# One scan per pair of channels over all 1024 tokens, and products by C of 8 tokens by 8 pairs

## The chip, the cores and the metric

The kernel runs on one core of one Trainium2 chip. The metric is the device time of one execution in microseconds, the median of several runs. Engines: TensorE (PE) multiplies and loads its weights (PEld), VectorE (DVE), ScalarE (ACT), GpSimd (POOL), and SyncE (SP), whose queue issues all DMAs.

## The reference

Sixteen samples of 256 channels by 1024 tokens go through an attention layer and then a selective state-space layer. The change is inside the recurrence of the second:

```python
def step(h, inp):
    d_t, B_t, C_t, u_t = inp
    dA = jnp.exp(d_t[..., None] * A)
    h = dA * h + (d_t * u_t)[..., None] * B_t[:, None, :]
    y = jnp.einsum('bdn,bn->bd', h, C_t)
    return (h, y)
```

It runs over 1024 tokens for 512 channels with 64 states each. `y` then goes through a gate and an output projection.

## The kernel before

**Work and tiles.** The 128 partitions hold the 64 states of two channels, a pair. A sample's 512 channels are four groups `k` of 128, each of four `q` of 32 channels, each of 16 pairs. Tokens come in two stretches `t` of 512. A unit is two pairs (`i` from 0 to 7, `e` 0 and 1) over one stretch; 8 units are a block, 256 units a sample, 4096 all.

**One unit.** `load` brings `du` (delta times u), broadcast over the states, 6 units ahead, and B, C and the pieces of delta where they are due. `inputs` (L904) multiplies du by B on POOL, 4 ahead. `decay` (L913) spreads delta over the states with one matmul per pair, each into a PSUM bank, and L916 turns it into exponentials on ACT, 2 ahead. `scan` (L926) runs the recurrence on DVE, one instruction per pair, and writes a slot of the state buffer. In the second stretch a scan starts from the last column of the first, which L951 saved.

**One block.** `outputs` multiplies the 16 slots of a full state buffer by C. `cd` holds C, spread by L939 so that a 128x32 weight has 4 tokens by 2 channels in its own eight columns (its other columns are zero) and four such weights add into 32 output rows. Each matmul (L967) takes 4 tokens of 16 slots as 64 moving columns; four groups of rows `g` are filled in turn. The result holds all combinations of tokens, of which the equal ones are wanted: ACT copies it out (L974, `y2`), and `turned` (L955) picks them with matmuls by parts of the identity into the other half of the bank `yb`. ACT copies that (L981, `yo`) and SP stores it.

**Order.** PE, ACT, DVE and POOL run in the order of the program text. The loop over units issues, for unit n: load(n + 6), inputs(n + 4), the scans of n, decay(n + 2), a share of the side work (the next sample's attention and projections, the last sample's gate), one step of each generator in `running`, and, at `i` = 0, a new `outputs` for the block just done, with its first step. Before, a block's products take seven steps: 32 matmuls at `i` = 0, 16 at each of `i` = 1 to 6; at `i` = 7 the last turn and `yo`.

**Buffers.** Two state buffers h0 and h1 take turns from block to block. A buffer is taken anew, as one tile, by the first scan of a block, which so waits for all readers of its former content. `aps` has four PSUM banks for decays.

Of the kernel before, what the change touches and what calls it, by code (L numbers as in the profile page):

```python
# [19 lines left out]
P = 128  # L20
C = 256
KC = C // P
L = 1024
# [10 lines left out]
TB = 512  # L34
NT = L // TB
SLOTS = 16
UNITS = ND * NT * 4 * 8

# [14 lines left out]
def attention_then_scan_kernel(  # L53
# [35 lines left out]
    aps = pool("aps", 4, space=PSUM)  # L89
# [5 lines left out]
    alone = cycle((mm, aps, aps))  # L95
    beside = {"scan": False}

    def psum(name, dims=P):
        src = mm if beside["scan"] else next(alone)
        return src.tile([P, HL], F32, name=name, tag="mm" if src is mm else "a")[:dims]  # L100
# [4 lines left out]
    def psum3(name):  # L105
        src = next(three) if beside["scan"] else next(alone)
        return src.tile([P, HL], F32, name=name, tag={mm: "mm", accp: "av"}.get(src, "a"))
# [7 lines left out]
    def hs(h):  # L115
        return ts(h, HL)
# [63 lines left out]
    turn = const.tile([P, 4, 2, 16], F32, name="turn")  # L180
    grid = ident.rearrange("p (m e j) -> p e j m", e=4, j=2)
    for e in range(4):
        nc.vector.tensor_copy(turn[:, e], grid[:, e])
# [27 lines left out]
    cd = hst.tile([P, TB // 16, P], F32, name="cd", tag="cd")  # L211
# [376 lines left out]
    def scan_inputs(b):  # L588
# [154 lines left out]
        dus = dram.tile([ND * NT * P, TB], F32, name="dus", tag="dus")  # L743
        dpv = dps.rearrange("(k q e p x) t -> k p e q x t", k=ND, q=4, e=2, p=3)
        duv = dus.rearrange("(k t d) c -> k d t c", k=ND, t=NT)
# [21 lines left out]
        for d in range(ND):  # L767
# [17 lines left out]
            nc.sync.dma_start(duv[d], du.rearrange("d (t c) -> d t c", t=NT))  # L785
# [20 lines left out]
    def gate_and_store(b):  # L806
# [62 lines left out]
        (b, t, k, q, i)  # L869
        for b in range(B) for t in range(NT) for k in range(ND) for q in range(4) for i in range(8)  # L870
# [4 lines left out]
    def load(n):  # L875
        b, t, k, q, i = units[n]
        st = state[b]
        if (k, q, i) == (0, 0, 0):
            bt = blk.tile([P, TB], F32, name="bt", tag="bt")
            ct = blk.tile([P, TB], F32, name="ct", tag="ct")  # L880
            for v, lo in ((bt, 0), (ct, NS)):
                src = st["rows"][lo : lo + NS, ts(t, TB)]
                nc.sync.dma_start(v, src.unsqueeze(1).to_broadcast([NS, 2, TB]))
            blocks[b, t] = {"bt": bt, "ct": ct}
        if i == 0:
            pieces = blk.tile([P, TB], BF16, name="pieces", tag="pieces")
            for e in range(2):
                src = st["dps"][ds(((k * 4 + q) * 2 + e) * 48, 48), ts(t, TB)]
                nc.sync.dma_start(pieces[ds(64 * e, 48)], src)
            blocks[b, t, k, q] = pieces  # L890
        du = dutp.tile([P, 2, TB], F32, name="dub", tag="dub")
        src = st["dus"][ts(k * NT + t, P)].rearrange(
            "(q j i e) c -> q i j (e c)", q=4, j=2, i=8
        )[q, i]
        nc.sync.dma_start(
            du.rearrange("p e c -> p (e c)"),
            src.unsqueeze(0).to_broadcast([NS, 2, 2 * TB]),
        )
        loaded[n] = du

    def inputs(n):
        b, t = units[n][:2]
        v, bt = loaded[n], blocks[b, t]["bt"]
        nc.gpsimd.tensor_tensor(v, v, bt.unsqueeze(1).to_broadcast([P, 2, TB]), ALU.mult)  # L904

    def decay(n):
        b, t, k, q, i = units[n]
        pieces = blocks[b, t, k, q]
        decays[n] = [aps.tile([P, TB], F32, name="a", tag="a") for _ in range(2)]
        for e in (1, 0):  # L910
            a, r = decays[n][e], ds(64 * e, 48)
            w = pick[r, i].rearrange("p n j -> p (n j)")
            nc.tensor.matmul(a, w, pieces[r], start=True, stop=True)  # L913
        for e, a in enumerate(decays[n]):
            at = 64 * k + 16 * q + 2 * i + e
            nc.scalar.activation(a, a, AF.Exp, scale=acol[:, at : at + 1])  # L916

    def scan(n, e):
        b, t, k, q, i = units[n]
        if (i, e) == (0, 0):  # L920
            if (t, k, q) == (0, 0, 0):
                now["last"] = blk.tile([P, DI // 2], F32, name="last", tag="last")
            now["h", q % 2] = hst.tile([P, SLOTS, TB], F32, name=f"h{q % 2}", tag=f"h{q % 2}")
        at = 64 * k + 16 * q + 2 * i + e
        first = now["last"][:, at : at + 1] if t else 0.0
        nc.vector.tensor_tensor_scan(  # L926
            now["h", q % 2][:, 2 * i + e, :], decays[n][e], loaded[n][:, e, :], first,
            ALU.mult, ALU.add,
        )
        if e == 1:  # L930
            del decays[n], loaded[n]
# [3 lines left out]
    def spread_c(b, t, some):  # L935
        ct = blocks[b, t]["ct"].rearrange("p (a c e) -> p a c e", c=4, e=4)
        for c in some:
            for j in range(2):
                nc.scalar.activation(  # L939
                    cd[:, :, 40 * c + j : 40 * c + j + 7 : 2], ct[:, :, c],  # L940
                    AF.Identity, scale=par[:, j : j + 1],
                )
# [4 lines left out]
    def outputs(b, t, k, q):  # L947
        hbuf = now["h", q % 2]
        out4 = yb[:, 256:].rearrange("p (j a m e) -> p a e j m", a=2, j=2, e=4)
        if t == 0:  # L950
            nc.scalar.copy(now["last"][:, ds(64 * k + 16 * q, 16)], hbuf[:, :, TB - 1])  # L951
        def turned(half, y2):
            for e in range(4):
                for s in range(4):
                    nc.tensor.matmul(  # L955
                        out4[32 * s : 32 * s + 16, half, e],
                        y2[:, 64 * s + e : 64 * s + 64 : 4], turn[:, e],
                        start=True, stop=True,
                    )

        y2 = None
        for half in range(2):
            for s in range(4):
                for c in range(4):
                    for g in range(4):
                        at = 128 * s + 64 * half + 16 * g + 4 * c
                        nc.tensor.matmul(  # L967
                            yb[ts(g, 32), ts(s, 64)],
                            cd[:, at // 16, ts(c, 32)], hbuf[:, :, at : at + 4],
                            start=(c == 0), stop=(c == 3),  # L970
                        )
# [3 lines left out]
                if s == 0 and half == 1:  # L975
                    turned(0, y2)
                if (half, s) != (0, 0):
                    yield
        turned(1, y2)
        yo = blk.tile([P, 256], F32, name="yo", tag="yo")  # L980
        nc.scalar.copy(yo, yb[:, 256:])  # L981
        for _ in range(3):
            yield
        to = state[b]["ys"][ds(k * P + 32 * q, 32), ts(t, TB)].rearrange(
            "(j i) (s c) -> s i j c", j=2, s=4
        )
        for s in range(4):
            nc.sync.dma_start(  # L988
                to[s], yo[32 * s : 32 * s + 16].rearrange("p (j c) -> p j c", j=2)
            )  # L990
# [29 lines left out]
    for n, (b, t, k, q, i) in enumerate(units):  # L1020
# [114 lines left out]
```

## Time and profile before

| | us |
|---|---|
| median of 3 runs | 13334.93 (13334.85 to 13353.89) |
| span of the profiled execution | 13355.7 |
| first scan starts, last scan ends | 385, 13308 |
| TensorE clock granted (mean, 1 is full) | 0.790 |
| exponentials L916, busy | 5060.9 |
| products by B on POOL L904, busy | 9690.4 |
| products by C, L967: matmuls, weight loads, busy | 3207.6, 2525.7 |
| copies y2 (L974, 1024) and yo (L981, 512), busy | 385.3, 193.1 |

"Busy" is the time in which at least one instruction of the group ran. A group's line ends with the idle time of its engine just before these instructions, and what ended it. In the slices of the page each digit is a tenth of 40 equal stretches of the span:

```profile
PE   7687878878788787887878878787787877878788
DVE  3899999999999999999999999999999999999998
PEclk8886878878788687887878878797786878879755
```

The 40 slices look alike: after the first sample's preparation the same loop runs to the end.

### The profile page before, as it was taken

The page shows a single profiled execution, that of the slowest core. Times are in us where ns is not written, and L with a number is a line of the kernel's source. Part 1 is how long each engine was busy: PE and PEld are TensorE (multiplying, and loading weights), DVE is VectorE, ACT ScalarE, POOL GpSimd, SP SyncE. Part 2 cuts the span into 40 slices and gives each one's busy share as a digit, 9 for nine tenths or more (in the row PEclk, how much of TensorE's full clock was granted, in tenths as well). Part 3 has the DMA queues.
Part 4 walks back from the last instruction along what each step waited for, and adds up shares of the span by engine and source line. Part 5 has one row for each costly group of instructions (what it writes and reads, how often), then busy time and mean ns, then how long its engine had stood idle before and what let it go on. Part 6 is the DMA issues. An engine that isn't in the chain of part 4 may idle for free. (4 is left out here: it accounts for less than half of the span.)

```text
span 13355.7 us, 429794 instructions
## 1 busy us (share of the span) xinstructions
PE 10665.6 (80%) x186800; PEld 5305.6 (40%) x186800; DVE 12217.1 (91%) x11652; ACT 7891.8 (59%) x13941; POOL 9695.2 (73%) x4105
## 2 busy tenths in 40 slices
PE   7687878878788787887878878787787877878788
PEld 3243343433434334343344433444344343433444
DVE  3899999999999999999999999999999999999998
ACT  3565665656656566565665656566565665656654
POOL 0676777777777777777767767687786877767798
PEclk8886878878788687887878878797786878879755
DMA  1566666675666766666666666666666666676676
GB/s 59 191 212 229 197 210 221 212 236 194 220 219 200 232 200 215 217 205 230 205 216 213 206 225 209 230 210 207 220 215 235 200 208 218 207 233 199 216 253 220
DMA packets 1002092, 2820.53 MB, mean 211 GB/s; under 512 B 176194, under 2 KB 319811, under 8 KB 1000196
## 3 DMA queue, kind: packets, MB, share of 16 engines
q1 hardware_dynamic: 1000196, 2793.03, 62.9%
q8 instruction: 1460, 23.92, 0.7%
q14 instruction: 436, 3.57, 0.1%
HBM read 2513.82 MB, written 261.62 MB: 208 GB/s over the span
## 5 line engine op out<-in xcount | busy, mean ns | idle before, releaser
L904 POOL TENSOR_TENSOR dub<-dub,bt 128x1024 f32<-128x1024 f32 x4096 | 9690.4, 2382 | 3605.4 <-DMA dub<-dus 3139.7
L916 ACT ACTIVATE a<-a,acol 128x512 f32<-128x512 f32 x8192 | 5060.9, 659 | 4086.9 <-PE a L913 4075.1
L926 DVE TENSOR_TENSOR_SCAN h<-a,last,dub 128x512 f32<-128x512 f32 x4096 | 4934.2, 1262 | 180.4 <-POOL dub L904 56.0
L926 DVE TENSOR_TENSOR_SCAN h<-a,dub 128x512 f32<-128x512 f32 x4096 | 4691.0, 1203 | 346.1 <-issue 124.9
L913 PE MATMUL a<-pieces,pick 48*128 48x512 bf16 x8192 | 2941.0, 454 | 2011.5 <-DVE h L926 1929.4
L967 PEld LDWEIGHTS yb<-h,cd 128*32 128x32 f32 x131072 | 2525.7, 131 | 3234.3 <-issue 2194.3
L967 PE MATMUL yb<-h,cd 128*32 128x64 f32 x131072 | 3207.6, 255 | 214.7 <-ACT yo L981 103.1
L913 PEld LDWEIGHTS <-pick 48*128 48x128 bf16 x8192 | 501.6, 95 | 1446.0 <-issue 1166.2
L427 PE MATMUL s_ps<-k,q 32*64 32x512 f32 x4096 | 830.7, 614 | 97.4 <-DVE mx L408 97.4
L955 PEld LDWEIGHTS yb<-turn,y 128*16 128x16 f32 x32768 | 456.1, 121 | 550.1 <-ACT y L974 305.6
L974 ACT COPY y<-yb 128x256 f32<-128x256 f32 x1024 | 385.3, 376 | 474.1 <-PE yb L967 467.7
L955 PE MATMUL yb<-turn,y 128*16 128x32 f32 x32768 | 552.1, 215 | 133.7 <-ACT y L974 133.4
L408 DVE TENSOR_REDUCE mx<-s_ps 128x1 f32<-128x512 f32 x1024 | 644.8, 674 | 9.7 <-PE s_ps L427 9.7
L495 PE MATMUL st_ps<-sp 33*128 33x512 f32 x2048 | 625.6, 650 | 0.1
L483 PE MATMUL av<-pt,vv 128*64 128x512 f32 x2048 | 621.9, 688 | 4.6 <-ACT sums L472 3.3
L503 ACT ACTIVATE pt<-st_ps 128x512 f32<-128x512 f32 x1024 | 557.5, 607 | 57.5 <-PE st_ps L495 56.7
L680 PE MATMUL g_ps<-w,xp 128*128 128x256 f32 x1536 | 517.1, 482 | 0.0
L680 PEld LDWEIGHTS g_ps<-w,xp 128*128 128x128 f32 x1536 | 400.6, 327 | 201.2 <-issue 169.5
L427 PEld LDWEIGHTS s_ps<-k,q 32*64 32x64 f32 x4096 | 193.8, 130 | 708.5 <-DVE mx L408 701.3
L666 DVE SCALAR_TENSOR_TENSOR u<-up,cwh,u 128x1024 f32<-128x1024 f32 x192 | 420.6, 2191 | 24.5 <-ACT u L658 24.2
L852 PE MATMUL m_ps<-w,xs 128*128 128x256 f32 x1024 | 319.0, 461 | 11.9 <-DVE xs L827 11.9
L495 PEld LDWEIGHTS st_ps<-sp 33*128 33x128 f32 x2048 | 222.8, 200 | 195.5 <-issue 109.8
(139 smaller groups left out, 6972.8 us busy)
## 6 DMA issues: line engine op xcount, KB each, us to landing
dub<-dus SPq DMA_DIRECT2D x4096, 512.0 KB
dps<-pc SPq DMA_DIRECT2D x384, 128.0 KB
pieces<-dps SPq DMA_DIRECT2D x1024, 48.0 KB
xs<-in_x_dram SPq DMA_DIRECT2D x64, 512.0 KB
xs<-kept SPq DMA_DIRECT2D x64, 512.0 KB
zs<-z SPq DMA_DIRECT2D x64, 512.0 KB
ud<-u SPq DMA_DIRECT2D x64, 512.0 KB
dus<-du SPq DMA_DIRECT2D x64, 512.0 KB
```

What stands on the lines that cost most here:

```text
L408: nc.vector.tensor_reduce(mx[:, g, c, hf : hf + 1], s, AX.X, ALU.max)
L427: nc.tensor.matmul(waiting[g][0][ts(e, 64)], q4[r, ts(c, 64)], k4[r, hs(hf)], start=True, stop=True,)
L483: nc.tensor.matmul(av[ts(e, 2 * DH)], vv[j // (NJ // 2)][:, j % (NJ // 2), 2 * pair + e, :], pts[e], start=(j == 0), stop=(j == NJ - 1),)
L495: nc.tensor.matmul(s, ka[r, ts(j, P)], qa[r, hs(hf)], start=True, stop=True)
L503: nc.scalar.activation(pt, s, AF.Exp)
L680: nc.tensor.matmul(ps[:, ts(q, C)], xp[k][:, ds(first + t, P, 4)], wg_s[:, k, t, :], start=(k == 0 and t == 0), stop=False,)
L904: nc.gpsimd.tensor_tensor(v, v, bt.unsqueeze(1).to_broadcast([P, 2, TB]), ALU.mult)
L913: nc.tensor.matmul(a, w, pieces[r], start=True, stop=True)
L916: nc.scalar.activation(a, a, AF.Exp, scale=acol[:, at : at + 1])
L926: nc.vector.tensor_tensor_scan(now["h", q % 2][:, 2 * i + e, :], decays[n][e], loaded[n][:, e, :], first, ALU.mult, ALU.add,)
L955: nc.tensor.matmul(out4[32 * s : 32 * s + 16, half, e], y2[:, 64 * s + e : 64 * s + 64 : 4], turn[:, e], start=True, stop=True,)
L967: nc.tensor.matmul(yb[ts(g, 32), ts(s, 64)], cd[:, at // 16, ts(c, 32)], hbuf[:, :, at : at + 4], start=(c == 0), stop=(c == 3),)
```

## The change

A unit becomes one pair over all 1024 tokens. Its decays lie in a tile of two PSUM banks, and one exponential and one scan (from 0) take both. The units of a `q` come as two blocks of 8, `e` = 0 and 1, and a state buffer holds 8 slots of 1024 tokens, the same bytes. The start column and its copy go. B and C of a sample are one load each into single buffers. A product by C takes 8 tokens of 8 slots, again 64 columns, two of them adding instead of four. A block's products take 4 rounds `r` of 4 `s`, two `s` a step, so eight steps of 16 matmuls; `y2` is copied four times per block, each `turned` call issues 8 matmuls for one output row group of 32, and the last `turned` and `yo` come in the step after, ahead of the next block's first products. The store has 8 DMAs for 4.

```diff
@@ -31,10 +31,8 @@
 CONV = 4
-TB = 512
-NT = L // TB
-SLOTS = 16
-UNITS = ND * NT * 4 * 8
+SLOTS = 8
+UNITS = ND * 4 * 2 * SLOTS
@@ -86,25 +84,35 @@
     dram1 = pool("dram1", 1, space=DRAM)
-    aps = pool("aps", 4, space=PSUM)
+    aps = pool("aps", 2, space=PSUM)
     yps = pool("yps", 1, space=PSUM)
-    alone = cycle((mm, aps, aps))
     beside = {"scan": False}
+    alone, spare = cycle((mm, aps)), []
+    def bank(src, name):
+        return src.tile([P, HL], F32, name=name, tag="mm" if src is mm else "av")
+    def free_bank(name):
+        if spare:
+            return spare.pop()
+        if next(alone) is mm:
+            return bank(mm, name)
+        both = aps.tile([P, L], F32, name=name, tag="a")
+        spare.append(both[:, hs(1)])
+        return both[:, hs(0)]
     def psum(name, dims=P):
-        src = mm if beside["scan"] else next(alone)
-        return src.tile([P, HL], F32, name=name, tag="mm" if src is mm else "a")[:dims]
+        return (bank(mm, name) if beside["scan"] else free_bank(name))[:dims]
     def psum3(name):
-        src = next(three) if beside["scan"] else next(alone)
-        return src.tile([P, HL], F32, name=name, tag={mm: "mm", accp: "av"}.get(src, "a"))
+        return bank(next(three), name) if beside["scan"] else free_bank(name)
@@ -177,10 +185,10 @@
-    turn = const.tile([P, 4, 2, 16], F32, name="turn")
-    grid = ident.rearrange("p (m e j) -> p e j m", e=4, j=2)
-    for e in range(4):
-        nc.vector.tensor_copy(turn[:, e], grid[:, e])
+    turn = const.tile([P, 8, 2, 8], F32, name="turn")
+    grid = ident.rearrange("p (m x j) -> p x j m", x=8, j=2)
+    for c in range(8):
+        nc.vector.tensor_copy(turn[:, c], grid[:, c])
@@ -208,7 +216,7 @@
-    cd = hst.tile([P, TB // 16, P], F32, name="cd", tag="cd")
+    cd = hst.tile([P, L // 16, 64], F32, name="cd", tag="cd")
     nc.gpsimd.memset(cd, 0.0)
@@ -740,9 +748,8 @@
         dps = dram.tile([ND * 3 * P, L], BF16, name="dps", tag="dps")
-        dus = dram.tile([ND * NT * P, TB], F32, name="dus", tag="dus")
+        dus = dram.tile([DI, L], F32, name="dus", tag="dus")
         dpv = dps.rearrange("(k q e p x) t -> k p e q x t", k=ND, q=4, e=2, p=3)
-        duv = dus.rearrange("(k t d) c -> k d t c", k=ND, t=NT)
@@ -782,7 +789,7 @@
                 nc.vector.tensor_tensor(du[:, hs(hf)], us[d][:, hs(hf)], ps, ALU.mult)
-            nc.sync.dma_start(duv[d], du.rearrange("d (t c) -> d t c", t=NT))
+            nc.sync.dma_start(dus[ts(d, P), :], du)
             yield 1.1
@@ -866,128 +873,110 @@
     units = [
-        (b, t, k, q, i)
-        for b in range(B) for t in range(NT) for k in range(ND) for q in range(4) for i in range(8)
+        (b, k, q, e, i)
+        for b in range(B) for k in range(ND) for q in range(4) for e in range(2) for i in range(SLOTS)
     ]
     def load(n):
-        b, t, k, q, i = units[n]
+        b, k, q, e, i = units[n]
         st = state[b]
-        if (k, q, i) == (0, 0, 0):
-            bt = blk.tile([P, TB], F32, name="bt", tag="bt")
-            ct = blk.tile([P, TB], F32, name="ct", tag="ct")
+        if (k, q, e, i) == (0, 0, 0, 0):
+            bt = hst.tile([P, L], F32, name="bt", tag="bt")
+            ct = hst.tile([P, L], F32, name="ct", tag="ct")
             for v, lo in ((bt, 0), (ct, NS)):
-                src = st["rows"][lo : lo + NS, ts(t, TB)]
-                nc.sync.dma_start(v, src.unsqueeze(1).to_broadcast([NS, 2, TB]))
-            blocks[b, t] = {"bt": bt, "ct": ct}
+                src = st["rows"][lo : lo + NS, :]
+                nc.sync.dma_start(v, src.unsqueeze(1).to_broadcast([NS, 2, L]))
+            blocks[b] = {"bt": bt, "ct": ct}
         if i == 0:
-            pieces = blk.tile([P, TB], BF16, name="pieces", tag="pieces")
-            for e in range(2):
-                src = st["dps"][ds(((k * 4 + q) * 2 + e) * 48, 48), ts(t, TB)]
-                nc.sync.dma_start(pieces[ds(64 * e, 48)], src)
-            blocks[b, t, k, q] = pieces
-        du = dutp.tile([P, 2, TB], F32, name="dub", tag="dub")
-        src = st["dus"][ts(k * NT + t, P)].rearrange(
-            "(q j i e) c -> q i j (e c)", q=4, j=2, i=8
-        )[q, i]
-        nc.sync.dma_start(
-            du.rearrange("p e c -> p (e c)"),
-            src.unsqueeze(0).to_broadcast([NS, 2, 2 * TB]),
+            pieces = blk.tile([P, HL], BF16, name="pieces", tag="pieces")
+            rows = ds(((k * 4 + q) * 2 + e) * 48, 48)
+            for hf in range(2):
+                nc.sync.dma_start(pieces[ds(64 * hf, 48)], st["dps"][rows, hs(hf)])
+            blocks[b, k, q, e] = pieces
+        du = dutp.tile([P, L], F32, name="dub", tag="dub")
+        src = st["dus"][ts(k, P)].rearrange("(q j i e) c -> q e i j c", q=4, j=2, i=SLOTS)[q, e, i]
+        nc.sync.dma_start(du, src.unsqueeze(0).to_broadcast([NS, 2, L]))
+        loaded[n] = du
+    def inputs(n):
+        v = loaded[n]
+        nc.gpsimd.tensor_tensor(v, v, blocks[units[n][0]]["bt"], ALU.mult)
+    def decay(n):
+        b, k, q, e, i = units[n]
+        pieces = blocks[b, k, q, e]
+        a = decays[n] = aps.tile([P, L], F32, name="a", tag="a")
+        for hf in (1, 0):
+            r = ds(64 * hf, 48)
+            w = pick[r, i].rearrange("p n j -> p (n j)")
+            nc.tensor.matmul(a[:, hs(hf)], w, pieces[r], start=True, stop=True)
+        at = 64 * k + 16 * q + 2 * i + e
+        nc.scalar.activation(a, a, AF.Exp, scale=acol[:, at : at + 1])
+    def scan(n):
+        b, k, q, e, i = units[n]
+        if i == 0:
+            now["h", e] = hst.tile([P, SLOTS, L], F32, name=f"h{e}", tag=f"h{e}")
+        nc.vector.tensor_tensor_scan(
+            now["h", e][:, i, :], decays.pop(n), loaded.pop(n), 0.0, ALU.mult, ALU.add
         )
-        loaded[n] = du
-    def inputs(n):
-        b, t = units[n][:2]
-        v, bt = loaded[n], blocks[b, t]["bt"]
-        nc.gpsimd.tensor_tensor(v, v, bt.unsqueeze(1).to_broadcast([P, 2, TB]), ALU.mult)
-    def decay(n):
-        b, t, k, q, i = units[n]
-        pieces = blocks[b, t, k, q]
-        decays[n] = [aps.tile([P, TB], F32, name="a", tag="a") for _ in range(2)]
-        for e in (1, 0):
-            a, r = decays[n][e], ds(64 * e, 48)
-            w = pick[r, i].rearrange("p n j -> p (n j)")
-            nc.tensor.matmul(a, w, pieces[r], start=True, stop=True)
-        for e, a in enumerate(decays[n]):
-            at = 64 * k + 16 * q + 2 * i + e
-            nc.scalar.activation(a, a, AF.Exp, scale=acol[:, at : at + 1])
-    def scan(n, e):
-        b, t, k, q, i = units[n]
-        if (i, e) == (0, 0):
-            if (t, k, q) == (0, 0, 0):
-                now["last"] = blk.tile([P, DI // 2], F32, name="last", tag="last")
-            now["h", q % 2] = hst.tile([P, SLOTS, TB], F32, name=f"h{q % 2}", tag=f"h{q % 2}")
-        at = 64 * k + 16 * q + 2 * i + e
-        first = now["last"][:, at : at + 1] if t else 0.0
-        nc.vector.tensor_tensor_scan(
-            now["h", q % 2][:, 2 * i + e, :], decays[n][e], loaded[n][:, e, :], first,
-            ALU.mult, ALU.add,
-        )
-        if e == 1:
-            del decays[n], loaded[n]
-    def spread_c(b, t, some):
-        ct = blocks[b, t]["ct"].rearrange("p (a c e) -> p a c e", c=4, e=4)
-        for c in some:
-            for j in range(2):
-                nc.scalar.activation(
-                    cd[:, :, 40 * c + j : 40 * c + j + 7 : 2], ct[:, :, c],
-                    AF.Identity, scale=par[:, j : j + 1],
+    def spread_c(b, c):
+        ct = blocks[b]["ct"].rearrange("p (a c x) -> p a c x", c=2, x=8)
+        for j in range(2):
+            nc.scalar.activation(
+                cd[:, :, 48 * c + j : 48 * c + j + 15 : 2], ct[:, :, c],
+                AF.Identity, scale=par[:, j : j + 1],
+            )
+    def outputs(b, k, q, e):
+        hbuf = now["h", e]
+        def turned(r, y2):
+            some = yb[ds(32 * (r // 2), 32), 256:].rearrange("p (j a m x) -> p a x j m", j=2, a=2, m=8)
+            for x in range(8):
+                nc.tensor.matmul(
+                    some[:, r % 2, x], y2[:, x : 256 : 8], turn[:, x], start=True, stop=True
                 )
-    def outputs(b, t, k, q):
-        hbuf = now["h", q % 2]
-        out4 = yb[:, 256:].rearrange("p (j a m e) -> p a e j m", a=2, j=2, e=4)
-        if t == 0:
-            nc.scalar.copy(now["last"][:, ds(64 * k + 16 * q, 16)], hbuf[:, :, TB - 1])
-        def turned(half, y2):
-            for e in range(4):
-                for s in range(4):
-                    nc.tensor.matmul(
-                        out4[32 * s : 32 * s + 16, half, e],
-                        y2[:, 64 * s + e : 64 * s + 64 : 4], turn[:, e],
-                        start=True, stop=True,
-                    )
         y2 = None
-        for half in range(2):
+        for r in range(4):
             for s in range(4):
-                for c in range(4):
+                for c in range(2):
                     for g in range(4):
-                        at = 128 * s + 64 * half + 16 * g + 4 * c
+                        at = 256 * s + 64 * r + 16 * g + 8 * c
                         nc.tensor.matmul(
                             yb[ts(g, 32), ts(s, 64)],
-                            cd[:, at // 16, ts(c, 32)], hbuf[:, :, at : at + 4],
-                            start=(c == 0), stop=(c == 3),
+                            cd[:, at // 16, ts(c, 32)], hbuf[:, :, at : at + 8],
+                            start=(c == 0), stop=(c == 1),
                         )
                     nc.scalar.copy(y2, yb[:, :256])
-                if s == 0 and half == 1:
-                    turned(0, y2)
-                if (half, s) != (0, 0):
+                if s == 1 and r > 0:
+                    turned(r - 1, y2)
+                if s % 2 == 1:
                     yield
-        turned(1, y2)
+        turned(3, y2)
         yo = blk.tile([P, 256], F32, name="yo", tag="yo")
-        nc.scalar.copy(yo, yb[:, 256:])
+        nc.scalar.copy(yo[:64], yb[:64, 256:])
         for _ in range(3):
             yield
-        to = state[b]["ys"][ds(k * P + 32 * q, 32), ts(t, TB)].rearrange(
-            "(j i) (s c) -> s i j c", j=2, s=4
+        to = state[b]["ys"][ds(k * P + 32 * q, 32)].rearrange(
+            "(j i e) (s h c) -> e h s i j c", j=2, e=2, s=4, h=2
         )
-        for s in range(4):
-            nc.sync.dma_start(
-                to[s], yo[32 * s : 32 * s + 16].rearrange("p (j c) -> p j c", j=2)
-            )
+        for h in range(2):
+            for s in range(4):
+                nc.sync.dma_start(
+                    to[e, h, s], yo[ds(32 * h + 8 * s, 8)].rearrange("p (j c) -> p j c", j=2)
+                )
@@ -1017,7 +1006,7 @@
     side, rate, due = iter(()), 1.0, 0.0
-    for n, (b, t, k, q, i) in enumerate(units):
+    for n, (b, k, q, e, i) in enumerate(units):
         at = n % UNITS
@@ -1039,8 +1028,7 @@
             inputs(n + LEAD)
-        scan(n, 0)
-        scan(n, 1)
+        scan(n)
         if n + 2 < len(units):
@@ -1050,12 +1038,12 @@
                 running.remove(g)
+        if n % UNITS in (SLOTS - 1, SLOTS):
+            spread_c(b, n % UNITS - SLOTS + 1)
         if i == 0 and n > 0:
             running.append(g)
-        if (k, q) == (0, 0) and i in (6, 7):
-            spread_c(b, t, ((0, 1), (2, 3))[i - 6])
     for g in running:
```

## The prediction

> **What bounds the kernel now.** I read the page's busy shares first, then the groups by line, then what the scans waited for, then stretches of the timeline.
>
> ```profile
> span 13355.7 us, 429794 instructions
> PE 10665.6 (80%) x186800; PEld 5305.6 (40%) x186800; DVE 12217.1 (91%) x11652; ACT 7891.8 (59%) x13941; POOL 9695.2 (73%) x4105
> ```
>
> VectorE (DVE) is busy 91% of the span; what it waits for is what sets the end. TensorE (PE) at 80% is second. The profiled execution (13355.7 us) is 0.16% above the median of the runs (13334.9); my sum is made against it, and 21 us come off at the end.
>
> ```profile
> L926 DVE TENSOR_TENSOR_SCAN h<-a,last,dub 128x512 f32<-128x512 f32 x4096 | 4934.2, 1262 | 180.4 <-POOL dub L904 56.0 <-issue 54.8 <-PE yb L967 42.8
> L926 DVE TENSOR_TENSOR_SCAN h<-a,dub 128x512 f32<-128x512 f32 x4096 | 4691.0, 1203 | 346.1 <-issue 124.9 <-PE yb L967 105.0 <-POOL dub L904 70.6
> L287 DVE TENSOR_TENSOR gn<-gn,gn_v_ps 128x1024 f32<-128x1024 f32 x32 | 38.6, 1209 | 10.2 <-ACT gn_v_ps L284 10.2
> L327 DVE TENSOR_TENSOR xn<-xn,ln_v 128x512 f32<-128x512 f32 x128 | 81.3, 677 | 62.8 <-ACT ln_v L322 62.8
> L955 PE MATMUL yb<-turn,y 128*16 128x32 f32 x32768 | 552.1, 215 | 133.7 <-ACT y L974 133.4 <-issue 0.3
> L457 PE MATMUL v_ps<-w,xn 128*128 128x128 f32 x512 | 75.3, 308 | 0.0
> L457 PEld LDWEIGHTS v_ps<-w,xn 128*128 128x128 f32 x512 | 68.9, 217 | 30.8 <-PE a L913 13.5 <-ACT y L974 13.2 <-issue 3.3
> L258 PEld LDWEIGHTS gn_v_ps<-gn_q,avg 128*128 128x128 f32 x128 | 32.0, 310 | 58.9 <-issue 46.5 <-DVE gn_q L253 9.3
> ```
>
> The two L926 lines are the scans: 9625 us of 12217. Starts against ends of all 4096 units in the trace give a mean of 2.383 us from the first scan of a unit to the end of its second, 0.77 us to the next unit (0.68 of it other DVE work) and 3.156 us from unit to unit, 25.25 us for 8. Scans already waited for the products by C ("PE yb L967", 42.8 + 105.0 us = 148 us, 126 times).
>
> **Scans.** A unit's two 512-token scans become one of 1024. No scan of that width is in the trace. The L327 and L287 lines double the width from 677 to 1209, so an instruction has about 145 ns that don't grow. Taken off the scan without a start column, (1203 - 145) x 2 + 145 = 2.26 us. A start column cost 59 ns and goes. Ends: all of the duration grows, 2 x 1.203 less the 58 ns by which neighbours overlap (4691.0 us / 4096 is 1.145), 2.35; or 160 ns are fixed (the 128x16 TENSOR_SCALAR of L270 took 0.16 us in all), 2.25. I take 2.26, as the rows that differ only in width give it: (2.383 - 2.26) x 4096 = -500 us (from -135 to -545).
>
> **The wait that is added.** Both versions keep two state buffers, and the first scan of a block rewrites the one used two blocks before, so it waits for that block's last products. Before, products ran at i = 0 (32) and i = 1 to 6 (16 each), and i = 7 was a spare unit. Now there are eight steps of 16, the last at i = 7. In PE's queue that step stands behind the decay matmuls of the unit, which wait for the scan just before, and behind the unit's share of the next sample's matmuls. So DVE must sit idle from the end of one scan until PE has done all of that. A light unit before:
>
> ```profile
> 5008.41 2.45 DVE L926 TENSOR_TENSOR_SCAN h<-a,last,dub 128x512 f32<-128x512 f32 x2
> 5010.92 0.58 PE L913 MATMUL a<-pieces,pick 48*128 48x512 bf16 x1 [0.59 <-DVE h L926]
> 5011.43 1.08 PE L967 MATMUL yb<-h,cd 128*32 128x64 f32 x32
> 5011.89 2.45 DVE L926 TENSOR_TENSOR_SCAN h<-a,last,dub 128x512 f32<-128x512 f32 x2
> ```
>
> The scan ends at 5010.86, the products at 5012.51, and the next scan started at 5011.89: had it to wait, it would lose 0.6 us. A heavy one:
>
> ```profile
> 2502.47 2.45 DVE L926 TENSOR_TENSOR_SCAN h<-a,last,dub 128x512 f32<-128x512 f32 x2
> 2505.27 3.65 PE L566 MATMUL f_ps<-xn,w 128*128 128x512 f32 x4
> 2505.95 2.45 DVE L926 TENSOR_TENSOR_SCAN h<-a,last,dub 128x512 f32<-128x512 f32 x2
> 2508.85 0.65 PE L967 MATMUL yb<-h,cd 128*32 128x64 f32 x32
> ```
>
> Here the products end at 2509.50, 3.55 us after the next scan's start. Over all units with i = 1 to 6, products end 2.83 us after their unit's scan and the next scan begins after 0.76; the mean of the overrun, counted as zero where there is none, is 2.16 us. There are 512 blocks, 510 of which wait: +1102 us, less the 148 us of such waits that there are: **+954 us**. Low end: PE began the second decay matmul 0.49 us late on average, and without that backlog the overrun is 1.6 us, +668. Queued behind the waiting scan are DVE's later side work, and behind that scan the next decay matmul on PE and its exponential.
>
> **Turning the products.** The 32 matmuls (64 instructions) per block of L955 stay as many, with 32 weight columns and 16 moving ones instead of 16 and 32. But four in a row went to four groups of output rows (32*s); now eight in a row go to one group (32*(r//2)). Before: 0.47 to 0.65 us per half in the timeline, 552.1/512 = 1.1 us per block. The new form is not in the trace. Ends for one weight load with its matmul: L457 has 128-wide pairs in one group at 68.9/512 = 135 ns per load, back to back: a quarter, 34 ns; L258 has short moving operands behind a wait, 32.0/128 = 250 ns per load, a quarter 63 ns, with 20 for the matmul 83. I take 50, nearer to the back-to-back row: 16 x 50 = 0.8 us per turn, 3.2 us per block, +2.1 us (0.54 to 1.33 us per turn: +1.1 to +4.2).
>
> The Trainium skill ("TensorE: Matmul & The Clock Gate", Part 3) says that weight loads overlap running matmuls only where the row group differs, which speaks against this change, since all these use all rows. Here L457 disagrees: its matmuls take 75.3/512 = 147 ns and its loads 135 ns each in the same time, so they overlap with the row group unchanged. By the rule a pair would be the sum of the two, near the upper of my ends, and the total some 600 us higher.
>
> **The copy ahead of the next products.** The copy of the turned half (yo) moves from i = 7 into the same step as the next block's first products. These share its bank and wait for it even now, with a unit between:
>
> ```profile
> PEld yb L967 <- ACT yo L981: 334.7, 215, 4.0
> ```
>
> One copy (377 ns at L981) and two handoffs: +0.7 us of PE per block, more if ScalarE (ACT) is behind.
>
> **What of PE's extra reaches DVE.** A unit's PE work before, second decay matmul to last product or turn, is about 2.55 us, 20.4 per block. It becomes 20.4 + 2.1 + 0.7 = 23.2. DVE's units take 2.26 + 0.71 = 2.97, 23.8 for eight. PE's spare falls from 3.4 to 0.6 us, so in uneven units (0.6 to 4 us) PE will often arrive late at i = 7, and the new wait grows by this. Between none and all of the 2.8 us extra; I take 0.7 x 510 = **+357 us**.
>
> **What costs nothing.** ACT: an exponential of 1024 is 659 ns and the 418 ns by which a 1024-wide ACTIVATE (1056, L274) exceeds a 512-wide one (638, L304), 1.08 against a pair's 1.24; 4096 x 0.16 = 655 us go. Twice as many y copies bring 1024 x 376 ns = 385 us, the 256 "last" copies take 58 us away, the spreading of C becomes 64 wider instructions for 256 of 406 ns. ACT is idle 41% of the span; were its cover gone it would gain. The exponential for unit n+2 still has a unit in hand. GpSimd (POOL): the same 4096 instructions. B and C become one buffer per sample: B's load waits until POOL's last product of the old sample, and POOL stands through one load (0.5 MB, 2.5 us at the page's 211 GB/s, and its latency). POOL ends 11.3 us (mean) ahead of the scan that needs it, which hides this; uncovered it is some 5 us x 15 samples. I put +30. SyncE issues 8 stores per block instead of 4, at 0.49 us +2 us in 25, three units after their copy, so nothing waits behind them. Loads are the same in number and size.
>
> **Sum.** 13356 - 500 + 954 + 357 + 30 = 14197; less 21: **14180 us**, 6% slower.
>
> **Rivals.** *PE becomes the bound.* If a pair costs 100 ns, as L258's loads suggest if they scale badly, a block has 6.4 us of turning: PE 20.4 - 1.1 + 6.4 + 0.7 = 26.4, then the first scan of the next block, which starts only after it, 2.4 with handoffs: 28.8 for 25.25, x 512 = +1820: 15150. For it: one output group; against it: L457.
>
> *The new wait is short and the scans win.* If the loads of side work fall so that at i = 7 products end as early as in the light unit (0.6 us over), the wait costs 306 - 148 = +158, no backlog forms, and 13356 - 500 + 158 + 30 - 21 = 13020. It decides below (500 + 148)/510 = 1.27 us. Against it: the mean is 2.16, and PE gets more work, not less.
>
> *Gain and loss cancel*, within 0.2% (27 us; what a measurement of this kernel can hardly tell from no change): a wait of about 1.25 us in all.
>
> **How the numbers follow.** Forecast 0.78, PE-bound 0.12, short wait 0.06, cancelling 0.04. The forecast's own range: all low ends, 13356 - 545 + 668 - 21 = 13460; upper, turning at 1.33 us per turn, PE 20.4 - 1.1 + 5.3 + 0.7 + 2.4 = 27.7 a block at the least, uneven units adding to that, 14600 to 14900. I give 13700 to 14850, which leaves out the PE-bound and short-wait cases and little else. Slower 0.90, same 0.04, faster 0.06.
>
> **What would show it.** 4096 scans near 2.26 us; idle before scans put down to PE yb of some 1400 to 1600 us in about 500 waits of 2 to 3 us each; L955 busy three times what it was; products waiting for yo at about every block. It is wrong if the waits for PE are short, if the 1024-wide scan isn't 2.25 to 2.35, or if PE is busy above 90%.

## The result, and the profile after

The changed kernel takes 15684.5 us (median of 4 runs, 15663.8 to 15708.1) against 13343.5 for the kernel before: a ratio of 1.1755, 95% interval 1.1738 to 1.1773, 2341 us slower. The direction was forecast; the time lies outside the range of 13700 to 14850.

The page of the changed kernel, its head, and the slices of the granted TensorE clock:

```profile
span 15706.0 us, 430046 instructions
PE 12119.9 (77%) x186800; PEld 7304.2 (47%) x186800; DVE 11806.3 (75%) x7560; ACT 7635.3 (49%) x10421; POOL 9749.9 (62%) x4105
PEclk8776777767677676776767767677676877767756
```

No engine is near full now. DVE's work fell by 411 us and its idle time rose from 1138 to 3900. PE is busy 1454 us longer, at a mean granted clock of 0.725 for 0.790. So the loss lies in engines that wait for each other, and the question is where.

The groups of the scans, the turns and the products:

```profile
L922 DVE TENSOR_TENSOR_SCAN h<-a,dub 128x1024 f32<-128x1024 f32 x4096 | 9238.5, 2279 | 3031.0 <-ACT a L916 1458.8 <-PE yb L955 1058.5 <-POOL dub L905 148.5
L945 PE MATMUL yb<-turn,y 128*32 128x16 f32 x32768 | 2317.3, 216 | 32.5 <-ACT y L962 31.4 <-issue 1.2
L955 PE MATMUL yb<-h,cd 128*32 128x64 f32 x131072 | 3530.5, 266 | 549.1 <-ACT yo L969 334.2 <-ACT y L962 193.9 <-ACT cd L931 17.6
```

The scan is as forecast (2279 ns for 2.26 us). The turns are busy 2317 us for 552. Scans wait 1059 us for the products by C (before 148), and 1459 us for their exponentials, where they hardly ever did (22.9 us; from the list of waits before, total, times, longest):

```profile
DVE h L926 <- ACT a L916: 22.9, 30, 1.1
```

Scan by scan, the mean time from the end of the scan of each unit `i` of a block to the start of the next unit's (DVE idle or at its other work), in us. The experiments that rows 3 to 5 belong to follow below:

| kernel | 0 | 1 | 2 | 3 | 4 | 5 | 6 | 7 | sum | scan(s) of a unit |
|---|---|---|---|---|---|---|---|---|---|---|
| before | 0.66 | 0.71 | 0.96 | 0.68 | 0.91 | 0.68 | 0.62 | 0.96 | 6.18 | 2.383 |
| after | 0.48 | 0.60 | 2.32 | 1.11 | 1.39 | 0.91 | 0.80 | 3.87 | 11.47 | 2.279 |
| eight steps put into before | 0.49 | 0.57 | 1.68 | 0.97 | 1.01 | 0.75 | 0.63 | 3.20 | 9.31 | 2.385 |
| seven steps put into after | 0.64 | 0.78 | 1.20 | 0.91 | 1.09 | 0.95 | 0.74 | 1.53 | 7.85 | 2.278 |
| the same, turns over four groups | 0.64 | 1.05 | 1.06 | 0.64 | 1.03 | 0.75 | 0.66 | 1.24 | 7.06 | 2.276 |

The difference of the two profiles, 2350 us, splits so: scans (2.279 - 2.383) x 4096 = -426; the edge of a block (after i = 7) 2.90 x 511 = +1483; the other gaps 2.39 x 512 = +1223; the first scan starts at 448 us for 385, and the tail is 6 us longer, +69.

The edge of a block in the timeline of the changed kernel, the scan of i = 7 and the next block's first:

```profile
5003.01 2.28 DVE L922 TENSOR_TENSOR_SCAN h<-a,dub 128x1024 f32<-128x1024 f32 x1
5005.34 0.39 PE L914 MATMUL a<-pieces,pick 48*128 48x512 bf16 x2 [1.94 <-DVE h L922]
5005.66 3.64 PE L660 MATMUL u_ps<-xp,w 128*128 128x512 f32 x4
5009.23 0.65 PE L955 MATMUL yb<-h,cd 128*32 128x64 f32 x32
5010.05 2.29 DVE L922 TENSOR_TENSOR_SCAN h<-a,dub 128x1024 f32<-128x1024 f32 x1 [3.59 <-PE yb L955]
```

It is the wait that was predicted: decay, side work, the last products, then the scan, 4.76 us after the one before (1.25 us of it another DVE instruction). Over all blocks, decay begins 1.34 us after the scan, products 1.57 later, take 0.79, and the scan follows after 0.19. Further on in the same block:

```profile
5022.90 2.29 DVE L922 TENSOR_TENSOR_SCAN h<-a,dub 128x1024 f32<-128x1024 f32 x1 [0.73 <-ACT a L916]
5023.27 0.65 PE L955 MATMUL yb<-h,cd 128*32 128x64 f32 x32
5023.74 1.11 PE L945 MATMUL yb<-turn,y 128*32 128x16 f32 x16
5024.79 0.39 PE L914 MATMUL a<-pieces,pick 48*128 48x512 bf16 x2
5025.22 1.09 ACT L916 ACTIVATE a<-a,acol 128x1024 f32<-128x1024 f32 x1 [2.42 <-DVE h L922]
5026.41 2.29 DVE L922 TENSOR_TENSOR_SCAN h<-a,dub 128x1024 f32<-128x1024 f32 x1 [1.22 <-ACT a L916]
```

This is what was not predicted. The scan that frees the decay tile ended at 5022.17 (it began at 5019.89). PE comes to the decay only at 5024.79, behind products and a turn; the exponential ends at 5026.31, and the scan after next, which should start at 5025.19, waits 1.22 us. PE's lateness now goes straight into DVE.

### The profile page after: what moved, and what is told of

The parts are those of the page before. It is cut to its first block, busy times and chain, and to the rows that moved or that the text cites. A ratio compares the mean times of both kernels' runs of the same rounds, so it can differ in the third digit from the quotient of the medians.

```text
span 15706.0 us, 430046 instructions
## 1 busy us (share of the span) xinstructions
PE 12119.9 (77%) x186800; PEld 7304.2 (47%) x186800; DVE 11806.3 (75%) x7560; ACT 7635.3 (49%) x10421; POOL 9749.9 (62%) x4105
## 5 line engine op out<-in xcount | busy, mean ns | idle before, releaser
L922 DVE TENSOR_TENSOR_SCAN h<-a,dub 128x1024 f32<-128x1024 f32 x4096 | 9238.5, 2279 | 3031.0 <-ACT a L916 1458.8
L916 ACT ACTIVATE a<-a,acol 128x1024 f32<-128x1024 f32 x4096 | 4464.5, 1090 | 5315.2 <-PE a L914 5266.9
L914 PE MATMUL a<-pieces,pick 48*128 48x512 bf16 x8192 | 2054.2, 494 | 2669.0 <-DVE h L922 2578.7
L955 PEld LDWEIGHTS yb<-h,cd 128*32 128x32 f32 x131072 | 2713.8, 138 | 2812.5 <-issue 1522.2
L955 PE MATMUL yb<-h,cd 128*32 128x64 f32 x131072 | 3530.5, 266 | 549.1 <-ACT yo L969 334.2
L945 PEld LDWEIGHTS yb<-turn,y 128*32 128x32 f32 x32768 | 2222.6, 158 | 479.8 <-issue 269.5
L945 PE MATMUL yb<-turn,y 128*32 128x16 f32 x32768 | 2317.3, 216 | 32.5 <-ACT y L962 31.4
L962 ACT COPY y<-yb 128x256 f32<-128x256 f32 x2048 | 764.7, 373 | 1229.2 <-PE yb L955 1213.0
L491 PE MATMUL av<-pt,vv 128*64 128x512 f32 x2048 | 757.6, 828 | 2.2 <-ACT sums L480 1.6
L969 ACT COPY yo<-yb 64x256 f32<-64x256 f32 x512 | 187.0, 365 | 481.6 <-PE yb L945 398.4
```

What stands on the lines that cost most here:

```text
L491: nc.tensor.matmul(av[ts(e, 2 * DH)], vv[j // (NJ // 2)][:, j % (NJ // 2), 2 * pair + e, :], pts[e], start=(j == 0), stop=(j == NJ - 1),)
L914: nc.tensor.matmul(a[:, hs(hf)], w, pieces[r], start=True, stop=True)
L922: nc.vector.tensor_tensor_scan(now["h", e][:, i, :], decays.pop(n), loaded.pop(n), 0.0, ALU.mult, ALU.add)
L945: nc.tensor.matmul(some[:, r % 2, x], y2[:, x : 256 : 8], turn[:, x], start=True, stop=True)
L955: nc.tensor.matmul(yb[ts(g, 32), ts(s, 64)], cd[:, at // 16, ts(c, 32)], hbuf[:, :, at : at + 8], start=(c == 0), stop=(c == 1),)
L962: nc.scalar.copy(y2, yb[:, :256])
```

## The experiments

Theory A: PE is overfull, above all by turns in one output group. Theory B: the decay tile of two banks leaves the exponentials too little lead. Theory C: the state buffer's wait at the block's edge is nearly all. Each time is a median beside runs of the kernel before on the same chip (13339 to 13351 us), with the ratio and its 95% interval.

**No turns.**

```diff
-                if s == 1 and r > 0:
-                    turned(r - 1, y2)
...
-        turned(3, y2)
```

> The changed kernel without the turning matmuls (the eight per round at one output row group); yo then copies the unused half of the bank, so the scans' result is missing from the output. Theory A (PE is overfull, the turns above all, and exponentials and scans wait for it): turns were busy 2317 us, 4.5 us per block; without them PE has its spare back, the scans' waits for the exponentials (1459 us) all but go, the wait for the last products falls to about 1000 us: 13700 to 14200. Theory B (a decay tile of two banks, with one exponential of 1024, leaves too little lead): the waits for exponentials stay above 1000 us, 15000 or more. Theory C (the wait for the state buffer at each block's edge is nearly all of it): 15100 or more.

Measured: 14567.9 us, 1.0914 (1.0898 to 1.0931). The scans and what they waited for:

```profile
L922 DVE TENSOR_TENSOR_SCAN h<-a,dub 128x1024 f32<-128x1024 f32 x4096 | 9216.0, 2277 | 2059.4 <-ACT a L916 802.4 <-PE yb L955 762.1 <-POOL dub L905 166.4
```

The turns are worth 1117 us, nearly half of the loss; no theory's figure held. 9% remains without them, so A alone falls, and waits for exponentials below 1000 us speak against B as the main cause.

**Seven steps in the changed kernel.**

```diff
-                if s % 2 == 1:
+                if s % 2 == 1 and (r, s) != (0, 1):
                     yield
```

> The changed kernel with the products in seven steps as before (32 at i = 0, the last 16 at i = 6, the last turn and yo at i = 7), so the first scan of a block has a spare unit again. Theory C: the waits for products fall from 1059 us to below 200 and the time to 13000 to 13600. Theory A: the waits for products go, but PE keeps its 4.5 us of turns per block and goes on making exponentials late: 14300 to 15000. Theory B: 14300 to 14900 with the waits for exponentials unchanged or larger.

Measured: 13842.8 us, 1.0366 (1.0350 to 1.0381), clock 0.793. In the list of waits of this kernel (total, times, longest):

```profile
DVE h L922 <- ACT a L916: 725.2, 673, 8.2
DVE h L922 <- PE yb L955: 234.9, 151, 6.7
```

One condition takes back 1842 of 2341 us; it brings the last turn and the copy back to i = 7 as well. Waits for products fall to 235 us, and those for exponentials halve, though turns and tiles are as they were: half of them came from the order of the steps too. C is nearest, some 250 us off.

**Eight steps in the kernel before.**

```diff
-                if (half, s) != (0, 0):
-                    yield
+                yield
```

> The kernel before with the products in eight steps of 16, the last at i = 7, and the last turn and yo in the next step ahead of the next products: the added wait and the moved copy alone, with scans, exponentials and turns as before. By the prediction's terms +954 us for the wait and a few hundred for the copy: 14200 to 14500. Theory C: +1800 or more, above 15100. Theory A: PE keeps 3 us of spare per block here, so 14000 to 14500, with waits for exponentials small.

Measured: 14954.2 us, 1.1208 (1.1180 to 1.1235), clock 0.728. With the old scans, exponentials and turns, the order of the steps alone costs 1605 us, more than the prediction's terms and A allowed and somewhat less than C. What sat before the scans, of the kernel so changed:

```profile
  PE yb L967: 623.8, 264
  issue: 455.2, 344
  POOL dub L904: 368.3, 177
  ACT a L916: 304.9, 99
```

The table above says more than these names: the gap at the edge grew from 0.96 to 3.20 us, and the one after i = 2 from 0.96 to 1.68, as in the changed kernel but smaller.

**One output group at a time in the kernel before.**

```diff
-            for e in range(4):
-                for s in range(4):
+            for s in range(4):
+                for e in range(4):
```

> The kernel before with the loops of its turns swapped, so that four matmuls in a row (eight instructions) go to the same output row group and not to four in turn; nothing else. If pairs in one group take some 60 ns as in the changed kernel, the 64 instructions of a block take 3 to 4 us for 1.1. Theory A: this eats the spare of 3.4 us and little more: 13500 to 14100, and the busy time of the turns goes from 552 us to 1500 to 2000. Theories B and C: PE has room, within 1% of 13340. If only the width of the weights matters and not the group, the busy time stays near 552.

Measured: 13288.5 us, 0.9949 (0.9933 to 0.9966), clock 0.815. The line of the turns:

```profile
L955 PE MATMUL yb<-turn,y 128*16 128x32 f32 x32768 | 1058.4, 214 | 135.4 <-ACT y L974 135.2
```

The group does matter: 1058 us for 552, 32 ns for an instruction that took 17. But here this is paid for by PE's spare, as B and C had it, and the kernel is even 0.5% faster, which no theory had.

**Turns over four groups, in seven steps.** The four rounds keep their own `y2`, and at i = 7 the matmuls go to four groups in turn; four copies bring them to the old layout of `yo`.

```diff
...
+            some = yb[:, 256:384].rearrange("p (j m x) -> p x j m", j=2, m=8)
             for x in range(8):
-                nc.tensor.matmul(
-                    some[:, r % 2, x], y2[:, x : 256 : 8], turn[:, x], start=True, stop=True
-                )
+                for r, y2 in enumerate(y2s):
+                    nc.tensor.matmul(
+                        some[ts(r, 32), x], y2[:, x : 256 : 8], turn[:, x], start=True, stop=True
+                    )
...
```

> The changed kernel in seven steps, with all turns of a block at i = 7 and the four rounds' matmuls going to four output row groups in turn (four y2 buffers, four copies into yo of the same layout); nothing is left out. Seven steps alone gave 13843 us, with the turns busy 2314. Theory A (turns in one group crowd PE): turns busy 500 to 800, and 12700 to 13250, below the kernel before, since the wider scan then shows its 420 us or so. Theory B (the two-bank decay tile leaves no lead): the waits for exponentials stay near 725 us and the time within 150 of 13843. If the strided weights and not the row group make a turn slow, its busy time stays above 1800 us.

Measured: 13434.6 us, 1.0065 (1.0048 to 1.0082). Two lines of its groups:

```profile
L923 DVE TENSOR_TENSOR_SCAN h<-a,dub 128x1024 f32<-128x1024 f32 x4096 | 9210.8, 2276 | 911.2 <-ACT a L917 490.2 <-POOL dub L906 192.8 <-PE yb L957 157.4
L947 PE MATMUL yb<-turn,y 128*32 128x16 f32 x32768 | 613.6, 217 | 140.6 <-ACT y L964 137.8
```

With the same weights and the same stride the turns fall from 2314 to 614 us: with the swapped loops above, which change the order alone, this shows that it was the group. Against seven steps alone 408 us are saved, the turns' move to i = 7 included; neither theory's time held. And the kernel isn't faster than the one before: 490 us of waits for exponentials stay.

**Seven steps and no turns.** Both edits of the first two runs together.

> The changed kernel in seven steps and without any turning matmuls (the scans' result is missing from the output): what the pair scans and two-bank decays give when neither the edge wait nor the turns are there. Theory A: 12600 to 13000. Theory B: 13400 to 13900 with 500 us or more of waits for exponentials.

Measured: 13341.9 us, 0.9993 (0.9983 to 1.0003). Its scans:

```profile
L922 DVE TENSOR_TENSOR_SCAN h<-a,dub 128x1024 f32<-128x1024 f32 x4096 | 9208.0, 2276 | 900.1 <-ACT a L916 466.9 <-POOL dub L905 186.3 <-PE yb L955 177.4
```

Even with no turning work at all the wider scan gains nothing. Turns are worth 501 us here and 1117 with eight steps: what PE loses counts double where the spare unit is gone. The waits that stay lie a little below what B had asked for, and the time between the two forecasts.

**The late copy alone in the kernel before.**

```diff
+        yield
         turned(1, y2)
         yo = blk.tile([P, 256], F32, name="yo", tag="yo")
```

> The kernel before with its seven steps of products left as they are, and only the last turn and the yo copy moved one step on, to i = 0 of the next block, ahead of that block's first 32 products: the moved copy without the added wait. The eight steps (both) cost 1605 us. If the edge wait is most of that: 13450 to 13800 here. If the copy is most of it: 14300 or more.

Measured: 13749.7 us, 1.0294 (1.0274 to 1.0314). In its list of waits the copy now stops PE 510 times in 512 blocks:

```profile
PE yb L967 <- ACT yo L982: 681.7, 510, 6.2
```

The edge is the larger part, as the first forecast had it: of the 1605 us of the eight steps some 400 are the copy and, by difference, 1205 the edge. The gaps agree. With the copy alone only the one after i = 2 grows, from 0.96 to 1.77 us (415 us over 512 blocks), and the other seven stay within 0.03 us: PE's delay at i = 0 reaches DVE two units later, as a late decay. With eight steps the gap at the edge grows by 2.24 us (1145 us over 511 edges).

**Half decays in seven steps.**

```diff
-        a = decays[n] = aps.tile([P, L], F32, name="a", tag="a")
+        decays[n] = [aps.tile([P, HL], F32, name="a", tag="a") for _ in range(2)]
...
+        h, v = now["h", e][:, i, :], loaded.pop(n)
+        for hf, a in enumerate(decays.pop(n)):
+            nc.vector.tensor_tensor_scan(
+                h[:, hs(hf)], a, v[:, hs(hf)], h[:, HL - 1 : HL] if hf else 0.0, ALU.mult, ALU.add
+            )
...
```

> The changed kernel in seven steps, with the decays of a unit in two one-bank tiles of four, two exponentials and two scans of 512 (the second starts from the last column of the first), as in the kernel before. Seven steps alone gave 13843 us. Theory B: the smaller tiles give the lead back, the waits for exponentials (725 us) go, and in spite of 0.1 us more of scan per unit (430 us) the time is 13300 to 13700. Theory A: the lead doesn't matter, the scans cost their 430 us: 14000 to 14400. The first scan starts near 385 us if the two-bank tiles made the preparation of the first sample slower, near 420 if not.

Measured: 14536.7 us, 1.0888 (1.0864 to 1.0911). The scans of this kernel:

```profile
L921 DVE TENSOR_TENSOR_SCAN h<-a,h,dub 128x512 f32<-128x512 f32 x4096 | 5254.3, 1283 | 411.4 <-ACT a L913 4.6 <-DVE h L921 4.2 <-ACT yo L968 0.5
L921 DVE TENSOR_TENSOR_SCAN h<-a,dub 128x512 f32<-128x512 f32 x4096 | 4950.7, 1209 | 778.6 <-ACT a L913 389.1 <-PE yb L954 188.6 <-POOL dub L901 140.5
```

The run doesn't decide: a scan that starts from the column its neighbour has just written costs more than I had set, 2.592 us for the two against 2.278 for one, 1286 us in all. Of this 538 come back through smaller gaps (6.79 us a block for 7.85). Waits for exponentials fall from 725 to 394 us, but units are longer as well. The first scan starts at 374 us: the two-bank tiles had made the first sample's preparation slower.

**Paired tiles in the kernel before.**

```diff
-        decays[n] = [aps.tile([P, TB], F32, name="a", tag="a") for _ in range(2)]
+        both = aps.tile([P, 2, TB], F32, name="a", tag="a")
+        decays[n] = [both[:, e] for e in range(2)]
...
```

> The kernel before with the two decays of a unit in one tile of two banks (two tiles, not four of one bank), its two exponentials and two scans unchanged: both decay matmuls now wait for both scans, as in the changed kernel, and the preparation uses the banks as the changed kernel does. Theory B' (the tile of two banks alone takes the lead of the exponentials): waits for exponentials of 300 to 500 us, 13650 to 13900. Theory D (the lead goes because a single scan needs its whole exponential at its start, where the second half of a pair is needed 1.2 us later; the tile matters little): waits for exponentials below 100 us, 13350 to 13500, of which 35 to 63 are a later first scan.

Measured: 13634.6 us, 1.0228 (1.0202 to 1.0253). The tile alone costs 295 us, 265 between the two profiles: 49 in the later first scan (435 for 385) and 213 in the loop (25.66 for 25.24 us a block). The time is just below what B' asked for, but few waits are put down to exponentials, as D said:

```profile
DVE h L937 <- ACT a L927: 46.7, 42, 2.0
```

So neither theory fits whole. Part of the price is ACT's: two exponentials on one tile take 1.36 us, on two tiles 1.24.

**Turns twice in the kernel before.**

```diff
-            for e in range(4):
+            for e in (0, 1, 2, 3) * 2:
```

> The kernel before with every turning matmul issued twice, in four groups in turn as before (same results): +1.1 us of PE per block, about what the swapped loops cost (1058 for 552 us busy), which yet ran 0.5% faster at a granted clock of 0.815 for 0.790. If more PE work raises the granted clock and this is the gain: 13250 to 13320 at a clock of 0.80 or more. If the gain came from the order of the groups itself: 13350 to 13700.

Measured: 13370.1 us, 1.0019 (1.0007 to 1.0031), turns busy 892 us, clock 0.807. A higher clock, and no gain: 340 us more of turns, where the swapped loops have 506, bring nothing, so that more PE work made the swapped loops faster is unlikely. The time lies in the range of the second forecast, the order of the groups; by what way the order would help stays open.

## Why the prediction went wrong

**Right.** The sign, and the place of the added wait: the first scan of a block behind the last products, in the way the prediction traced it. Its size was a quarter low: +954 forecast; 1205 us by the two runs on the kernel before. The scan (-500; -426) and ACT's lighter load held. B's single buffer, put at +30, cost some 70: the gap at a sample's edge is 6.51 us, and 1.85 in the kernel before put into eight steps, x 15.

**The step that failed: "What of PE's extra reaches DVE", +357.** The +357 was PE's extra at the edge of a block (0.7 us x 510); inside a block the prediction put nothing. The profiles show +1223 us in the gaps inside a block, and at the edge 3.87 us where the first term makes 2.92 (0.76 + 2.16), +485. So the size at the edge was near, and the path that was left out, from a late PE by a late decay and exponential to the scan, is most of the miss. Three inputs were off, all in one direction.

*"The exponential for unit n+2 still has a unit in hand."* It hadn't. In the second of two scans the old kernel had a median of 1.8 to 2.6 us between the end of an exponential and its use (in the first 1.25 to 2.05); the changed kernel has 0.1 to 1.6 from i = 2 on, and in 27 to 52% of the scans from i = 3 on less than 0.15 us. A pair's second exponential is needed one scan later than the first, a wide scan needs all of it at once, and both halves of its tile wait for one whole scan. The paired tiles showed 213 us of it in the loop; that the rest lies in needing the whole exponential at once is argued from seven steps without turns (467 us of waits with neither the edge wait nor the turns), not shown by a run of its own.

*PE at i = 0.* I had put 0.8 us for a turn and 0.7 for the copy on top of the old 1.77 us from decay to products, 3.3 us. The mean is 3.91. A turn took 1.11 us; its instructions start 61 ns apart, where I took 50. The price by the rule of the Trainium skill ("TensorE: Matmul & The Clock Gate", Part 3) that I had set aside on the strength of L457 came nearer: the sum of load and matmul of that row makes 282/4 = 70 ns. L457's pairs start 112 ns apart, and a quarter of that, 28 ns, did not carry over to 32-wide groups. Whether the rule is the reason isn't shown: the turns start 60 ns apart where the granted clock is full and 62 where it is half, while the 16 products take 0.65 and 1.1 us. Also, PE idles at the block's edge while the first scan runs, and comes out of it at a low clock: granted are 0.56 in mean at the products of i = 0 and 0.84 at those of i = 7, and the 16 products take 1.07 and 0.79 us. Decays start 2.3 us after their unit's scan at i = 1 and 2 (the second decay before: 0.8 and 0.7), and the gap after i = 2 shows it.

*The sum over averages.* I set PE's 23.2 us against DVE's 23.8 and took it that units would even out. They can't: the wait for the state buffer makes DVE wait for PE once a block, as PE's decays wait for DVE, PE stands while DVE catches up, and then starts the next block late with the clock down. The runs show that the terms don't add: turns cost 501 us with a spare unit at the edge and 1117 without; on the kernel before, where PE has room, a swap that adds 506 us of turns costs nothing.

**The rival "PE becomes the bound"** named the nearest time (15150) with the wrong price, so by luck: pairs start 61 ns apart, not 100, and PE is busy 77%, not above 90. **Left out altogether**: the two-bank tiles delay the first scan by 35 to 63 us (420 to 448 for 385; 374 with one-bank tiles).

Adding up by runs, in the order in which they were made (another order would share it out differently): of 2341 us, 1842 go with the eighth step and the copy that moved with it, 408 more with the one output group, and 91 are left. In this last kernel the wide scan gains 438 us (2.276 for 2.383), and longer gaps (7.06 for 6.18 us a block, 450 us) and a first scan 61 us later use it up. No version with the wide scan beat the kernel before; the one that beats both kernels is the kernel before with the swapped turns, 13288.5 us (0.9949).

## What to carry to other kernels

When a reader of a double buffer moves one step closer to the writer that reuses it, price the whole queue in front of that reader, then ask what the stalled engine releases: here one spare step, with the copy that moved with it, was worth 12%, more than every other edit together. A longer instruction in place of two short ones also needs all of its input earlier and frees its buffer later; count the lead of the stage that feeds it, not only its own duration. Where an engine's spare sinks to a few per cent, don't add the extras: they are no longer hidden one by one.

## What the hardware showed unexpectedly

- Small matmuls that go to one output row group one after another kept PE busy 71 ns each (2314 us for 32768; 32 weight columns, 16 moving), and 19 (614 us) when four groups took turns; with 16 weight columns and 32 moving 32 ns for 17. The Trainium skill ("TensorEngine Tiling (Array Packing)", Key Properties) says that different tiles load weights and multiply in parallel; these runs agree, and show the price of not using it.
- The mean granted TensorE clock was lower where PE stood idle for most of the first scan of each block: 0.725, 0.728 and 0.741 in the profiles of the three kernels with eight steps (idle for 82 to 100% of it), 0.768 to 0.815 in those of the nine with seven (16 to 53%).
- A scan whose start column was written by the scan just before it: 2.592 us for the two, against 2.383 for the two scans of the kernel before, which don't depend on each other.
- Swapping the loops of the turns in the kernel before doubled their busy time and made the kernel 0.5% faster. Doubling the turns in four groups raised the clock too (0.807) without a gain, so the cause is open.
